# Self attention of a decoder layer: normalized tokens turned by way of memory and one VectorE turn

## The chip, the cores and the metric

The kernel runs on one core of a Trainium2 chip. The core has a matrix engine (TensorE, PE in the profile; its weight loads are listed as PEld), a vector engine (VectorE, DVE), an engine for activations and copies (ScalarE, ACT), a general engine (GpSimd, POOL) and an engine that issues transfers (SyncE, SP). Each works through its own instructions in order and waits on semaphores for the others. Tiles lie in on-chip memory of 128 partitions (SBUF); matrix products land in a second, small memory (PSUM), from which ACT or DVE must fetch them. Transfers between the chip's large memory and SBUF run on 16 DMA engines.

The metric is the device time of one execution in microseconds. Before the change it was 3776.5 us, the median of three runs (3776.08 to 3777.55).

## The reference

The program is one decoder layer in float32 over 32 batches of 128 tokens with 512 features: differential self attention, a cross attention, and a mixture of 32 experts with a shared expert. Only the first part is touched:

```python
x = x + attn(layernorm(x), Wq, Wk, Wv, Wo, lq1, lk1, lq2, lk2)
# attn: 16 heads, each with two halves of 16 features
q = (h @ Wq) * scaling; k = h @ Wk; v = h @ Wv      # h = layernorm(x)
aw = softmax(q k^T + causal)                        # 32 halves
aw = aw[first halves] - lam * aw[second halves]
out = rms_normalized(aw @ v) * (1 - LAMBDA_INIT) @ Wo
```

All three projections multiply the normalized tokens by weights, so they need the normalized tokens turned: features on the partitions, tokens along the free dimension (the tile `hT`).

## The kernel before

`self_attention` (L115) works in **steps**. A batch has two steps (`CP` = 2 of the four chunks of 128 features each); the loop at L478 runs step n over 64 (batch, half) pairs, with five more to drain. Every step holds pieces of several batches at once: for step n the maxima of the scores of step n (`maxima`), the exponentials of step n-1 (`turn_maxima`, `sums`, `exponentials`), the weighted values of step n-2 (`weigh`, `divide`), the projections of queries and keys for the next pair of batches (`queries_and_keys`, one of four chunks a step), and further pieces that alternate. In odd steps there are the projection to values for a later batch (`values`, L238 and the copy of v at L242) and, of batches two to three ahead, the shift by mean and deviation (`normalize`, L87 by way of `shifted`), the turn (`turn_in`, L199) and the next load of x (`load`, L151). In even steps there are the output projection (`leave`, L405, sum with x at L409, store at L410), the statistics of a later batch (`measure`: L56, L58, L60 on DVE, L62 and L66 on POOL), the mean squares of the heads (`norms`, L375 to L378) and the load of x for the residual (`load_again`, L398).

`turn_in` is done by TensorE: `turn4` takes a PSUM buffer, turns four 128 x 128 blocks against an identity (L95), and ACT copies the result to `hT` (L207). `hT` holds two batches and has two buffers. `queries_and_keys` (L220) and `values` (L238) read it.

All PSUM tiles come from one pool of four buffers (`banks`, L50), two banks each, handed out in the order of the claims: whoever claims a buffer waits until the last reader of the claim four earlier is done.

The order of the work: until `first.close()` (L476) every engine takes its instructions as written. Behind it a planner orders each engine's instructions: by their place in the program, among those that it takes to be ready by its own estimates of durations and transfers. The program can tie instructions with `tc.issue_after(ins)`: what is traced in that block on the engine of `ins` stays behind `ins` in that engine's order. `behind()` (L503) ties to the last reduction of the maxima (L264) of the step; `last_v` is the copy of v (L242). In the hardware each engine then keeps the planned order, whatever really comes late.

After self attention come the cross attention, its routing, the shared expert and the experts; their code stays as it is.

Of the kernel before, what the change touches and what calls it, by code (L numbers as in the profile page):

```python
# [10 lines left out]
F32 = mybir.dt.float32  # L11
# [7 lines left out]
P = 128  # L19
E = 512  # L20
EC = E // P
# [14 lines left out]
class Common:  # L36
# [49 lines left out]

        self.nc.scalar.activation(out, src, AF.Identity, bias=down, scale=rstd)  # L87

    def turn4(self, src, order=range(EC)):


        tr = self.banks()[:, 0, :].rearrange("p (c x) -> p c x", c=EC)
        cols = src.rearrange("p (c x) -> p c x", c=EC)
        for c, n in enumerate(order):
            self.nc.tensor.transpose(tr[:, c, :], cols[:, n, :], self.ident)  # L95
        return tr
# [15 lines left out]
            call(*args)  # L112


def self_attention(cm, x, x1_d, Wq, Wk, Wv, Wo, lq1, lk1, lq2, lk2, heads, heads_in, beside):  # L115

# [11 lines left out]
    nc, tc, bank = cm.nc, cm.tc, cm.banks  # L130
    B = x.shape[0]
    H, D, G = 16, 32, 2
    CP = 2
    ROW = (16, 0)
    with ExitStack() as ctx:
# [7 lines left out]
        pj2 = early.enter_context(tc.tile_pool(name="a_pj2", bufs=2))  # L143

        xin, xres = {}, {}

        def load(b, queue=nc.sync):

            if b < B:
                xin[b] = pj2.tile([P, E], F32, name="xin")  # L150
                queue.dma_start(out=xin[b], in_=x[b])  # L151
# [10 lines left out]
        for b in range(G):  # L162
            load(b, both[b % 2])
        w = {
            name: (wp if name == "wo" else pj).tile([P, EC, E], F32, name=name)
            for name in ("wk", "wq", "wv", "wo")
        }
        for oc in range(EC):
            for name, src, queue in (("wk", Wk, nc.sync), ("wq", Wq, both[oc < 2])):
                queue.dma_start(  # L170
                    out=w[name][:, :, ts(oc, P)],
                    in_=src[:, ts(oc, P)].rearrange("(c p) m -> p c m", p=P),
                )
            if oc == 0:
                nc.sync.dma_start(out=heads, in_=heads_in)
        vecs = wp.tile([P, 4, 16], F32, name="lam_vecs")
        for i, src in enumerate((lq1, lq2, lk1, lk2)):
            nc.sync.dma_start(out=vecs[:, i, :], in_=src.partition_broadcast(P))
        for name, src in (("wv", Wv), ("wo", Wo)):
            nc.sync.dma_start(out=w[name], in_=src.rearrange("(c p) m -> p c m", p=P))  # L180

        begun = wp.tile([P, 1], F32, name="a_begun")
        nc.scalar.activation(begun, cm.mhalf[:, 0:1], AF.Exp)
# [1 line left out]
        hT, qT, kz, k1, vs = {}, {}, {}, {}, {}  # L185
        last, last_v = {}, [None]
        h, sc_of, qm, expd, u, o, an = {}, {}, {}, {}, {}, {}, {}

        def measure(b):
            if b < B:  # L190
                h[b] = cm.moments(pj2, xin[b], "a_")

        def normalize(b):
            if b < B:
                rstd, down = h[b]
                h[b] = pj2.tile([P, E], F32, name="h")
                cm.shifted(h[b], xin.pop(b), rstd, down)

        def turn_in(b):  # L199

            if b >= B:
                return
            g, i = divmod(b, G)
            if i == 0:
                hT[g] = pj2.tile([P, EC, G * P], F32, name="hT")
            tr = cm.turn4(h.pop(b))
            nc.scalar.copy(hT[g][:, :, ts(i, P)], tr)  # L207

        def queries_and_keys(g, oc):

# [262 lines left out]
        for b in range(G):  # L473
            turn_in(G + b)
            load(2 * G + b)
        first.close()  # L476
        steps = [(b, cp) for b in range(B) for cp in range(EC // CP)]
        for n in range(len(steps) + 5):  # L478
            g, k = divmod(n, 2 * G)
            if n == len(steps) - 2 * G:  # L480
                early.close()
            at = {ago: steps[n - ago] for ago in range(6) if 0 <= n - ago < len(steps)}
            if 1 in at:
                turn_maxima(*at[1])
                sums(*at[1], 0)
            if 0 in at:
                maxima(*at[0])
            queries_and_keys(g + 1, k)
            if 1 in at:
                exponentials(*at[1])  # L490
                sums(*at[1], 1)
            if 2 in at:
                weigh(*at[2])
            if k % 2:
                values(g + 1, k // 2)
            elif 5 in at:
                leave(at[5][0])
            if 2 in at:
                divide(*at[2])
                if at[2][1]:  # L500
                    finish(at[2][0])

            def behind():  # L503

                return tc.issue_after(last[at[0]].ins) if 0 in at else nullcontext()

            b = (g + 2) * G + k // 2
            if k % 2 == 0:
                if 3 in at:
                    with behind():  # L510
                        norms(at[3][0])
                measure(b)
                if 4 in at:
                    load_again(at[4][0])
            else:
                normalize(b)
                turn_in(b)
                load(b + G)
                if 4 in at:
                    with behind():  # L520
                        scale_out(at[4][0])
                    turn_out(at[4][0])
            if n in beside:
                beside[n]()


class CrossAttention:
# [101 lines left out]
    def load(self, b):  # L629
        src = self.src  # L630
        src[b, "k"] = self.pi.tile([P, E], F32, name="cx")
        self.nc.sync.dma_start(out=src[b, "k"], in_=self.ctx_in[b])
        src[b, "q"] = self.pi.tile([P, E], F32, name="h2")
        self.nc.sync.dma_start(out=src[b, "q"], in_=self.x1_d[b])

    def measure(self, b):
        q = self.sided[b, "q", 0] = self.pi.tile([P, E], F32, name="xq0", bufs=2)
        self.scale[b] = self.cm.moments_by_sums(self.pi, self.src[b, "q"], q, "x_")
# [575 lines left out]
class Shared:  # L1214
# [4 lines left out]
    G = 4  # L1219
# [544 lines left out]
def decoder_kernel(  # L1764
# [5 lines left out]
    nc = tc.nc  # L1770
    B = x.shape[0]
# [14 lines left out]
    half_eid = const.tile([P, 2], I32, name="half_eid")  # L1786

    x1_d = dram.tile([B, P, E], F32, name="x1_d")
    h3_d = dram.tile([T, E], F32, name="h3_d")
    h3T_d = dram.tile([B, P, EC, P], F32, name="h3T_d")  # L1790
    table_ds = [dram.tile([(NX * B + 2) * P, 2], F32, name=f"table_d{i}") for i in range(2)]
# [6 lines left out]
    with tc.tile_pool(name="x_w", bufs=1, side="right") as x_w:  # L1798
        rest = x_w.tile([P, E], F32, name="rest")
        nc.gpsimd.memset(rest, 0.0)  # L1800
        routing = Routing(cm, x_w, table_ds, B)
        cross = CrossAttention(cm, x_w, x1_d, x2_d, h3_d, h3T_d, ctx_in, routing)
        cross.plan(lambda: s_w.load(), lambda: shared.load(0))
        x_ctx = ExitStack()

        def begin():
            cross.begin(
                x_ctx.enter_context(
                    tc.tile_pool(name="x_in", bufs=2, side="right", reuse_waits="tile")
                )  # L1810
            )
            cross.advance(7)

        n = 2 * B
        beside = {
            12: lambda: cross.load_weights(
                xWq, xbq, xWk, xbk, xWv, xbv, xWo, xbo, cos, sin, rotT, gate_w
            ),
            20: lambda: cross.prepare(heads),
            28: routing.prepare,  # L1820
            n - 4: begin,
        }

        for i, count in enumerate((4, 4, 5, 2, 2, 2, 2)):
            beside[n - 3 + i] = lambda count=count: cross.advance(count)
        self_attention(cm, x, x1_d, aWq, aWk, aWv, aWo, lq1, lk1, lq2, lk2, heads, heads_in, beside)
        s_w_pool = ctx.enter_context(tc.tile_pool(name="s_w", bufs=1, reuse_waits="tile"))
        s_w = SharedWeights(cm, s_w_pool, sw_gate, sw_up, sw_down)
        s_h_pool = ctx.enter_context(tc.tile_pool(name="s_h", bufs=2, reuse_waits="tile"))
        shared = Shared(cm, s_h_pool, h3T_d, sum_d, out)  # L1830
        x_out = ExitStack()
        p2 = x_out.enter_context(tc.tile_pool(name="x_p2", bufs=2, reuse_waits="tile"))
        cross.run(p2)
        x_ctx.close()
        s_pool = x_out.enter_context(tc.tile_pool(name="s_p", bufs=1, reuse_waits="tile"))
        shared.use(s_pool, s_w)
        en = mybir.EngineType
        in_order = {en.PE, en.DVE, en.Activation, en.Pool}
        todo = [lambda: cross.rest(2)] * 34 + [
            lambda: routing.tiles(eid, fresh, rows, used, usual, mixed),  # L1840
            lambda: routing.halves(half, half_eid),
            lambda: nc.sync.dma_start(out=sum_d[T : T + P, :], in_=rest),
        ]

        def between():
            if todo:
                todo.pop(0)()

        EARLY = 3
        with tc.manual_schedule(engines=in_order):
            for g in range(EARLY - 1):
                shared.group(g, False, between)
            while todo:
                between()
# [42 lines left out]
    for i in range(2):  # L1900
        b = done // 2
# [59 lines left out]
```

## Time and profile before

| what | us |
|---|---|
| median of 3 runs | 3776.5 |
| the profiled execution: time, span | 3776.16, 3774.4 |
| self attention, roughly | 0 to 750 |
| an odd and an even step (steps 7 to 56, but step 20) | 11.18 and 11.39 |
| steps 57, 58, 59 (no batch left to turn) | 10.75, 10.77, 10.75 |
| four turns on TensorE, start to the next work (L95) | 0.44 |
| copy of hT (L207), shift (L87) on ACT, each | 0.57, 0.81 |
| statistics of a batch on DVE (L56, L58, L60) | 0.69, 0.18, 0.15 |
| a turn of 32 x 32 blocks on DVE, 128 x 512 (L392) | 0.71 |

The length of a step is taken from the first L291 (the turn of the maxima, the first work of a step on TensorE) to the next step's. In the profile, busy time of an engine is the time that its instructions cover; the ends of matrix products are modelled, so a wait between two of them can hide in the busy time. Groups are named by line, engine, operation, and output and input tiles. "Idle before" is what the engine waited just before the instruction, and behind the arrow stands what ended the wait. The span is the time from the first to the last instruction of the program; the execution's own time is 1.8 us longer.

### The profile page before, as it was taken

To read this page: it belongs to the slowest core of one execution; us is meant where nothing else is said; L and a number is where in the kernel's file an instruction comes from. 1 tells how busy PE (TensorE), PEld (TensorE's weight loads), DVE (VectorE), ACT (ScalarE), POOL (GpSimd) and SP (SyncE) were. 2 spreads that over 40 slices of the span, in tenths; PEclk is the share of its full clock that TensorE was granted. 3 is DMA by queue.
4 is the path that set the end of the run, shared out by engine and by line. 5 is a ranking of instruction groups with operands and counts; after the bars stand their busy time and mean duration, and the time that the engine had idled before them with its cause. 6 is when DMAs were issued, how large, how long until landed. Compare 5 with 4: busy or idle time off the path is not lost. (4 is left out here: it accounts for less than half of the span.)

```text
span 3774.4 us, 62331 instructions
## 1 busy us (share of the span) xinstructions
PE 3693.1 (98%) x19828; PEld 1945.4 (52%) x19828; DVE 2600.8 (69%) x5594; ACT 2247.9 (60%) x6384; POOL 1921.4 (51%) x2154
## 2 busy tenths in 40 slices
PE   8999999889999999999999999999999999999999
PEld 5666666534444444444445555555555555555444
DVE  4888888877777878877425777777777777775111
ACT  6989999847667776766502555555555555554000
POOL 3555555545777777777423555555555555553000
PEclk9999999999999999999999999999999999999999
DMA  4111110121111111111125665656565665674210
GB/s 114 33 36 35 35 38 26 43 82 51 57 57 51 51 49 48 51 46 37 51 87 184 139 162 133 167 134 163 122 160 141 153 156 135 139 186 70 94 56 34
DMA packets 147715, 340.42 MB, mean 90 GB/s; under 512 B 28976, under 2 KB 33776, under 8 KB 147312
## 3 DMA queue, kind: packets, MB, share of 16 engines
q1 hardware_dynamic: 90560, 227.75, 18.6%
q0 software_dynamic: 55616, 107.79, 15.4%
q8 instruction: 160, 2.62, 0.3%
q14 instruction: 179, 1.47, 0.1%
q10 hardware_dynamic: 1200, 0.79, 0.1%
HBM read 574.59 MB, written 102.17 MB: 179 GB/s over the span
## 5 line engine op out<-in xcount | busy, mean ns | idle before, releaser
L694 DVE TENSOR_REDUCE nm<-ps 128x2 f32<-128x1024 f32 x512 | 611.0, 1215 | 113.1 <-PE ps L690 106.6
L717 ACT ACTIVATE xp<-ps 128x1024 f32<-128x1024 f32 x512 | 505.9, 1021 | 265.6 <-PE ps L690 203.0
L1688 POOL DMA_INDIRECT sum_d<-e_out,e_into x192 | 309.7, 1613 | 558.7 <-ACT e_out L1681 254.6
L713 PE MATMUL ps<-xqn,xk 32*128 32x512 f32 x2048 | 528.1, 621 | 20.6 <-ACT xp L717 19.2
L690 PE MATMUL ps<-xk,xq 32*128 32x512 f32 x2048 | 527.5, 631 | 0.8 <-DVE nm L694 0.7
L1593 DVE STREAM_TRANSPOSE e_xT<-e_xr 64x256 f32<-64x256 f32 x800 | 497.8, 622 | 17.4 <-issue 9.1
L1578 POOL DMA_INDIRECT e_xr<-h_d,e_run_of x400 | 415.2, 1038 | 161.1 <-issue 123.2
L1608 PE MATMUL ps<-wg,e_xT 128*128 128x352 f32 x1536 | 491.6, 463 | 0.0
L1608 PE MATMUL ps<-wu,e_xT 128*128 128x352 f32 x1536 | 485.7, 459 | 0.0
L1612 ACT ACTIVATE e_act<-ps 128x352 f32<-128x352 f32 x200 | 92.8, 464 | 575.2 <-PE ps L1608 553.8
L1608 PEld LDWEIGHTS ps<-wg,e_xT 128*128 128x128 f32 x1536 | 287.2, 190 | 229.3 <-issue 42.5
L278 ACT ACTIVATE s<-s,a_nm 128x128 f32<-128x128 f32 x1024 | 395.7, 395 | 5.1 <-DVE a_nm L264 5.1
L1649 ACT COPY e_mainT<-e_turned 32x64 f32<-32x64 f32 x1536 | 370.7, 241 | 20.2
L1643 DVE STREAM_TRANSPOSE e_mainT<-e_gu 32x64 f32<-32x64 f32 x1536 | 359.8, 234 | 24.6
L1608 PEld LDWEIGHTS ps<-wu,e_xT 128*128 128x128 f32 x1536 | 291.8, 190 | 162.6
L1660 PE MATMUL ps<-wd,e_mainT 128*128 128x512 f32 x768 | 361.9, 593 | 2.1 <-ACT e_mainT L1649 2.1
L1613 DVE TENSOR_TENSOR e_gu<-e_act,ps 128x352 f32<-128x352 f32 x200 | 104.2, 521 | 327.2 <-ACT e_act L1612 240.0
L713 PEld LDWEIGHTS ps<-xqn,xk 32*128 32x128 f32 x2048 | 169.1, 184 | 284.6 <-ACT xp L717 123.6
L728 PE MATMUL ps<-xp,v 128*32 128x512 f32 x2048 | 233.0, 595 | 7.9 <-ACT xp L717 7.4
L1031 POOL DMA_INDIRECT table_d<-entry,at x192 | 202.6, 1055 | 63.9 <-issue 53.1
L227 POOL TENSOR_SCALAR k<-kz,a_keep,a_extra 128x256 f32<-128x256 f32 x128 | 83.1, 659 | 286.8 <-ACT kz L226 286.8
L1272 ACT ACTIVATE s_act<-ps 128x512 f32<-128x512 f32 x40 | 23.9, 597 | 332.1 <-PE ps L1265 332.1
(315 smaller groups left out, 6189.9 us busy)
## 6 DMA issues: line engine op xcount, KB each, us to landing
wg<-in_L_ffn_w_gate_dram SPq DMA_DIRECT2D x192, 704.0 KB
wu<-in_L_ffn_w_up_dram SPq DMA_DIRECT2D x192, 704.0 KB
wd<-in_L_ffn_w_down_dram SPq DMA_DIRECT2D x192, 512.0 KB
wd_ends<-in_L_ffn_w_down_dram SPq DMA_DIRECT2D x192, 192.0 KB
xg<-in_L_ffn_w_gate_dram SPq DMA_DIRECT2D x16, 704.0 KB
xu<-in_L_ffn_w_up_dram SPq DMA_DIRECT2D x16, 704.0 KB
xd<-in_L_ffn_w_down_dram SPq DMA_DIRECT2D x16, 576.0 KB
xres<-in_x_dram SPq DMA_DIRECT2D x32, 256.0 KB
```

The source lines that it names most:

```text
L278: nc.scalar.activation(s[:, j, c, side, :], s[:, j, c, side, :], AF.Exp, bias=nm[n][:, side, at : at + 1], accum_out=sm[n][:, to : to + 1],)
L690: self.nc.tensor.matmul(sc[:, i, :], q[rows, ts(c, P)], k[rows, :], start=True, stop=True)
L694: self.nc.vector.tensor_reduce(at[:, self.ROW[side], 2 * pair : 2 * pair + 2], sc, AX.X, ALU.max, negate=True)
L713: self.nc.tensor.matmul(sc[:, i, :], k[rows, ts(c, P)], q[rows, :], start=True, stop=True)
L717: self.nc.scalar.activation(e, sc, AF.Exp)
L1578: self.cm.nc.gpsimd.indirect_dma_start(out=xr[:, t, :], out_offset=None, in_=self.h3_d.rearrange("t (h f) -> (t h) f", h=self.R), in_offse ...
L1593: self.cm.nc.vector.transpose(to[ts(w, half), :, v], xr[ts(v, half), w])
L1608: nc.tensor.matmul(pgu[lanes, half, 0:M], t[:, c, lanes], w[:, c, :], start=c == 0, stop=c == EC - 1,)
L1643: self.cm.nc.vector.transpose(t[ts(q, 32), 0:n, ts(s, 32)], cols[ts(s, 32)])
L1649: self.cm.nc.scalar.copy(t[ts(q, 32), 0:n, ts(s, 32)], z[ts(s, 32), k, 0:n])
L1660: mm(py, t[:, c, :], self.wd[i % SETS][:, c, :], start=c == 0, stop=False)
L1688: self.cm.nc.gpsimd.indirect_dma_start(out=self.sum_d[:, :], out_offset=bass.IndirectOffsetOnAxis(ap=into, axis=0), in_=y[:, :], in_offset ...
```

## The change

For batches 4 to 31 the turn no longer goes over TensorE. The shift (now in `send`) writes its result with two inner orders exchanged: of each 128 features, feature 4f + c goes to place 32c + f. The tile is stored to a new area `h_d` in memory and read back by four transfers, one for each 128 features and each into 32 partitions: partition 32q + i gets, for the four groups t of 32 tokens, the 128 features of quarter q of token 32t + i. One DVE instruction (`receive`) then turns each 32 x 32 block, and what comes out is `hT` with feature 4p + c on partition p in chunk c. So that this agrees with the weights, `wk`, `wq` and `wv` are now loaded with row 4p + c on partition p (`(p c) m` in place of `(c p) m`), and the first four batches, still turned on TensorE, are read with a step of four elements (`strided=True`).

The order changes too. `send(b + 1)` and its transfers stand in the odd step, tied on ACT behind the copy of v; `receive(b)` stands in the next even step, tied on DVE behind the maxima; the statistics `measure(b + 2)` move from the even to the odd step, tied on DVE behind the maxima; the load of x comes after the transfers of `send`. Before the loop, in the part that runs as written, the statistics of batches 4 and 5, the sending of batch 4 and a load are added.

```diff
-    def turn4(self, src, order=range(EC)):
+    def turn4(self, src, order=range(EC), strided=False):
...
-        cols = src.rearrange("p (c x) -> p c x", c=EC)
+        cols = src.rearrange("p (x c) -> p c x" if strided else "p (c x) -> p c x", c=EC)
...
-                    in_=src[:, ts(oc, P)].rearrange("(c p) m -> p c m", p=P),
+                    in_=src[:, ts(oc, P)].rearrange("(p c) m -> p c m", p=P),
...
-        for name, src in (("wv", Wv), ("wo", Wo)):
-            nc.sync.dma_start(out=w[name], in_=src.rearrange("(c p) m -> p c m", p=P))
+        nc.sync.dma_start(out=w["wv"], in_=Wv.rearrange("(p c) m -> p c m", p=P))
+        nc.sync.dma_start(out=w["wo"], in_=Wo.rearrange("(c p) m -> p c m", p=P))
...
-        def turn_in(b):
-
-            if b >= B:
-                return
+        def turned(b):
+
             g, i = divmod(b, G)
             if i == 0:
                 hT[g] = pj2.tile([P, EC, G * P], F32, name="hT")
-            tr = cm.turn4(h.pop(b))
-            nc.scalar.copy(hT[g][:, :, ts(i, P)], tr)
+            return hT[g][:, :, ts(i, P)]
+
+        def turn_in(b):
+            nc.scalar.copy(turned(b), cm.turn4(h.pop(b), strided=True))
+
+        def send(b):
+
+            if b >= B:
+                return
+            rstd, down = h[b]
+            t = pj2.tile([P, E], F32, name="h")
+            cm.shifted(
+                t.rearrange("p (q c f) -> p q f c", q=4, c=EC),
+                xin.pop(b).rearrange("p (q f c) -> p q f c", q=4, c=EC), rstd, down,
+            )
+            nc.sync.dma_start(out=h_d[b], in_=t)
+            h[b] = pj2.tile([P, 4, P], F32, name="h_runs")
+            for q in range(4):
+                nc.sync.dma_start(
+                    out=h[b][ts(q, 32)],
+                    in_=h_d[b][:, ts(q, P)].rearrange("(t i) r -> i t r", i=32),
+                )
+
+        def receive(b):
+
+            if b < B:
+                nc.vector.transpose(
+                    turned(b).rearrange("p c (t i) -> p c t i", i=32),
+                    h.pop(b).rearrange("p t (c f) -> p c t f", c=EC),
+                )
...
             turn_in(G + b)
             load(2 * G + b)
+        measure(2 * G)
+        send(2 * G)
+        load(3 * G)
+        measure(2 * G + 1)
         first.close()
...
-                measure(b)
+                with behind():
+                    receive(b)
                 if 4 in at:
                     load_again(at[4][0])
             else:
-                normalize(b)
-                turn_in(b)
-                load(b + G)
+                with tc.issue_after(last_v[0].ins):
+                    send(b + 1)
+                with behind():
+                    measure(b + 2)
+                load(b + 1 + G)
```

More of the change, by code (lines that the diff above doesn't have):

```diff
@@ L112, in run, with self_attention @@
             call(*args)
-def self_attention(cm, x, x1_d, Wq, Wk, Wv, Wo, lq1, lk1, lq2, lk2, heads, heads_in, beside):
+def self_attention(cm, x, x1_d, h_d, Wq, Wk, Wv, Wo, lq1, lk1, lq2, lk2, heads, heads_in, beside):
     nc, tc, bank = cm.nc, cm.tc, cm.banks
@@ L1788, in decoder_kernel @@
     x1_d = dram.tile([B, P, E], F32, name="x1_d")
+    h_d = dram.tile([B, P, E], F32, name="h_d")
     h3_d = dram.tile([T, E], F32, name="h3_d")
@@ L1825, in decoder_kernel @@
             beside[n - 3 + i] = lambda count=count: cross.advance(count)
-        self_attention(cm, x, x1_d, aWq, aWk, aWv, aWo, lq1, lk1, lq2, lk2, heads, heads_in, beside)
+        self_attention(cm, x, x1_d, h_d, aWq, aWk, aWv, aWo, lq1, lk1, lq2, lk2, heads, heads_in, beside)
         s_w_pool = ctx.enter_context(tc.tile_pool(name="s_w", bufs=1, reuse_waits="tile"))
```

## The prediction

> **What bounds the kernel now.** I read the page first, then stretches of self attention by engine, then its waits and its instructions in order of time. The page gives TensorE 98% of the span:
>
> ```profile
> PE 3693.1 (98%) x19828; PEld 1945.4 (52%) x19828; DVE 2600.8 (69%) x5594; ACT 2247.9 (60%) x6384; POOL 1921.4 (51%) x2154
> ```
>
> The chain that ended last covers only the last 290 us, so the stage has to be read by itself. Two steps of it (one batch), in the table by stretches; columns are length, then busy us of PE, PEld, DVE, ACT, POOL, then clock, DMA share, GB/s:
>
> ```profile
> 321.46:344.03 22.57, 22.57 (x187) 14.44 (x186) 18.88 (x28) 20.55 (x80) 11.60 (x13) 1.00 0.12 36
> ...
> 682.67:704.18 21.51, 21.51 (x183) 13.73 (x182) 18.14 (x25) 19.36 (x78) 10.94 (x11) 1.00 0.08 27
> ```
>
> PE has no gap in either. Each stretch runs from an odd step's first L291 to the next odd step's. In the first, which repeats with 22.57 us from step 7 to step 56 (step 20 apart, which holds other preparation), a batch is turned by PE; in the second no batch is left to turn, while projections, scores, values and output go on. So 21.51 us is what PE needs without the turn. The timeline of PE (start, length, line) shows where the 1.06 us lie:
>
> ```profile
> 306.19 3.60 PE L238 MATMUL ps<-wv,hT 128*128 128x512 f32 x8
> 309.63 0.60 PE L95 MATMUL ps<-ident,h 128*128 128x128 f32 x4
> 310.07 0.38 PE L291 MATMUL ps<-ident,a_nm 128*128 128x128 f32 x2
> 310.38 1.79 PE L251 MATMUL ps<-kz,qT 32*128 32x256 f32 x16
> 312.10 1.99 PE L220 MATMUL ps<-hT,wk 128*128 128x256 f32 x8
> ...
> 318.02 3.60 PE L405 MATMUL ps<-wo,anT 128*128 128x512 f32 x8
> 321.46 0.38 PE L291 MATMUL ps<-ident,a_nm 128*128 128x128 f32 x2
> 321.77 1.15 PE L251 MATMUL ps<-kz,qT 32*128 32x256 f32 x16
> ```
>
> The four turns take PE 0.44 us (309.63 to 310.07). Then the scores (L251) take 1.79 us instead of 1.15: the turn is a ninth claim on four PSUM buffers in a step that otherwise makes eight, so the scores wait for the copy of v and L220 for the copy of hT. Both copies, in ACT's timeline:
>
> ```profile
> 310.42 0.57 ACT L242 COPY v<-ps 128x512 f32<-128x512 f32 x1
> 310.88 0.64 ACT L368 ACTIVATE sq<-at 128x512 f32<-128x512 f32 x1
> 311.42 0.57 ACT L207 COPY hT<-ps 128x512 f32<-128x512 f32 x1
> ```
>
> hT ends at 311.99 and L220 starts at 312.10. "Busy" hides this wait, since a matmul's modelled end covers it.
>
> **The change part by part.** *Turns and hT copies leave.* 28 batches (4 to 31): 28 x 0.44 = 12.3 us of turns, 28 x 0.62 = 17.4 us of buffer waits; together 28 x 1.06 = 29.7 us. With eight claims a step, as in the second stretch, the scores wait for neither copy. ACT also loses 0.57 us a batch.
>
> *Moved on ACT: the shift.* It now follows the copy of v, hence (by program order) sq, at a step's border. It writes every 4 bytes to a new place 128 bytes on, which no ACT row shows. Low end 0.81 us (L87 as it is, and 0.80 in L87's other form, with two run orders exchanged); a gain below that I exclude, since the elements are as many. High end 1.44 us: L1593, a VectorE turn read 16 bytes apart, takes 630 ns for 256 elements, 2.46 ns each, against 711 ns for 512 at L392, 1.39 ns each: 0.81 x 1.77. I take 0.81, the same engine's row. The Trainium skill ("SBUF — State Buffer", section "Door 1: The DMA port swizzle") says that SBUF has 16-byte lines and that an access to a new line each time pays; it gives no price, so by it only the high end gains weight, and the L1593 row agrees in direction. Cover: ACT waits 2.02 us a batch for PE (before L226: 1.56 and 0.46), and in the second stretch's pattern 2.14 us; either end fits. Without that cover the shift costs PE its excess, up to 0.6 us a batch.
>
> *Moved on DVE: statistics.* L56, L58, L60 (0.69 + 0.18 + 0.15 = 1.03 us) go from the even step to the odd one, behind the maxima; behind them on DVE are an, anT, u and o, for which PE's buffers and POOL's L363 wait. In the second stretch DVE waits 0.94 us at the end of the odd step (L293 for L291), so it is 0.1 short; but the first o product takes 1.11 us there and 0.42 in the even step, and later it runs beside less of POOL's L318. I take 0; bounds 0 and 0.1 x 28 = 3 us. L56's wait for its load, 0.98 us here, goes, since that load now has two steps. POOL's two small operations (0.55 + 0.26) go along; POOL is idle half of the time.
>
> *Added on DVE: the turn.* L392 has its shape: 0.71 us; high end 2 x 0.63 = 1.26 if the exchanged order costs as at L1593; nothing below, it is the same work at least. I take 0.71, as both sides keep runs of 128 bytes. It comes in the even step, behind maxima and ms. DVE's busy time becomes 18.1 + 1.03 + 0.71 = 19.9 of 21.5 us.
>
> *Added on SP: one store and four reads, past x_d, xres and xin.* SP's waits show it idle most of the time, and what it issues has a step or more to spare (xres issued at 301.83 is used at 321.66). The chain counts: the store takes 2.03 us (L410 at 299.80; the load of xres that waits for it at 301.83), four issues 3 x 0.47 us (SP's issues at 8.91, 9.38, 9.86), the last read up to 2.46 us (L151 at 315.43, L56 starts 317.89): 5.9 us. Against an even step's L291 at 693.42: v ends +1.4, sq +1.9, shift +2.7, data +8.6 us. DVE reaches its turn at +6.9 (ms ends 700.31). If it waits there, the turn ends at +9.3 where u stood at +7.5: 1.8 us late. Behind u stand rs, o and L409, which waits 1.36 us for PE anyway:
>
> ```profile
> 700.95 0.85 DVE L339 STREAM_TRANSPOSE u<-ps 128x640 f32<-128x640 f32 x1 [0.43 <-PE ps L337]
> ...
> 702.54 0.48 DVE L352 SCALAR_TENSOR_TENSOR o<-u,nlam,rs 128x256 f32<-128x256 f32 x1
> 704.38 0.69 DVE L409 TENSOR_TENSOR xres<-xres,ps 128x512 f32<-128x512 f32 x1 [1.36 <-PE ps L405]
> ```
>
> So L409 is 0.4 us late, and PE needs its buffer only for L220 at 705.57, 0.5 us after it ends at 705.07: nothing is lost. If the planner puts the turn behind o, DVE does not wait. Bounds: 0, and with the shift at 1.44 us another 0.63, of which PE sees 0.55: 15 us. I take 1 us in all.
>
> *Start.* 16 turns now read 16 bytes apart, 3.3 us in all before: 0 more to 3.3 x 0.77 = 2.5; I take 1, between, as no PE row is near. Weights by "(p c)": wk and wq keep 512-byte runs; wv has landed when L238 starts right behind L220. Both 0. Shift and store of batch 4 come where ACT shifted it before (40.08). Steps 1 to 6 are irregular (70.8 us against 3 x 22.57): plus or minus 3 us, unpriced in the centre.
>
> The Trainium skill ("VectorE: DVE Perf Modes", section "Rules for kernel authors") speaks against the change: turn 128 x 128 on TensorE where PSUM may take the result. Taken as a time it would make the change cost 28 x (0.71 - 0.44) = 7.6 us. The row of PE without a gap decides otherwise: 0.71 us lie on an engine with waits.
>
> Sum: 29.7 - 1 - 1 = 27.7 us. The profiled execution took 3776.16 (span 3774.4 and 1.8 around it): 3748.5. It stands 0.3 under the median of 3776.5, so 3748.8.
>
> **Rivals.** (1) *The data come late and eat part of it.* As bounded above, 0.5 us a batch of PE wait behind L409: 14 us, 3763. For: L56 already waits 0.67 to 0.98 us for one load that the planner took to be there, and now there are two transfers in a row. Against: 1.36 + 0.5 us of slack. (2) *Slower: the shift falls behind the eight sums.* There it stood (L87 at 314.59, 4.5 us after L291) and data would be at 4.5 + 0.8 + 5.9 = 11.2. If the turn stays before u, it ends at +11.9, u is 4.4 late, L409 3.0, PE 2.5 us a batch: net 28 x (2.5 - 1.06) = 40 us, 3817. It decides once the data come after +9.7 (7.53 + 1.36 + 0.5 + 1.06 - 0.71), 1.1 us beyond my sum. Against: the statistics are now two steps old, so the shift is ready when v ends. (3) *Nothing is gained*, 3776: the steps without turn were short because statistics and shift were absent, too, and another engine takes PE's place. Against: ACT would have 20.0 and DVE 19.9 us in 21.5.
>
> **How the numbers follow.** Forecast 0.62 (3742 to 3753), rival 1 0.20 (3753 to 3769), rival 3 0.05, rival 2 0.13. A measurement tells about 0.2% (7.6 us) from no change, so faster is below 3769: 0.82; same 0.05; slower 0.13. For 8 in 10 the range goes from 3742, the early steps' 3 us and the start's costs on the good side, to 3770, through rival 1.
>
> **What would show it.** L291 to L291 of 10.75 in both steps; no L207 after the start; L251 at 1.15 in both; the shift right behind sq; the new turn at about 0.7 us and what DVE waits before it; L409's wait. Wrong if L220 of odd steps starts late behind L409 (rivals 1, 2), if ACT no longer waits before L226 (3), or if the shift is above 1.5 us.

## The result, and the profile after

The changed kernel takes 3815.85 us (median of 4 runs, 3814.38 to 3817.14), the kernel before 3776.73 beside it. The ratio is 1.0104, 95% interval 1.0091 to 1.0116: slower by 39 us. The forecast was 3748.8 us, the range 3742 to 3770. (Of all executions below, one of the kernel with the turn a step later took 6144.52 us at a granted clock of 0.556; the ratios leave it out.)

All of it lies in self attention: the first turn of the maxima (now L317) of step 57 starts at 723.82 us, before at 682.67, 41 us earlier. (Lines of the loop have moved by 26: L220 is L246, L251 L277, L318 L344, L352 L378, L405 L431, L409 L435. The new turn is L230, the store L219, the four reads L222.)

From the page, busy times of the engines; then one batch of the middle in the table by stretches (length, busy us of PE, PEld, DVE, ACT, POOL, clock, DMA share, GB/s):

```profile
PE 3677.3 (96%) x19716; PEld 1931.5 (51%) x19716; DVE 2659.2 (70%) x5622; ACT 2240.9 (59%) x6356; POOL 1916.7 (50%) x2154
```

```profile
507.00:531.31 24.31, 21.83 (x183) 13.80 (x182) 21.07 (x29) 20.29 (x79) 11.71 (x13) 1.00 0.18 56
```

TensorE works 21.83 us in the batch, less than the 22.57 of before, but the batch has become 24.31 us long: TensorE now has holes. The waits of the stretch from 120 to 640 us (total us, times, longest) name them:

```profile
DVE hT L230 <- DMA h_runs<-h_d: 54.0, 21, 3.6
...
POOL a_ln_rstd L62 <- DVE a_ln_ve L60: 33.5, 18, 2.0
...
PE ps L246 <- DVE xres L435: 30.0, 20, 1.6
ACT sq L394 <- POOL at L389: 26.6, 17, 1.6
...
PE ps L431 <- ACT qT L257: 14.5, 17, 0.9
```

VectorE waits for the turned-back data at L230 in front of the new turn, and TensorE then waits for L435, the sum with x. PE's timeline over the same batch shows where the two holes are, in the odd step (from 507.00) before L246 and in the even step (from 519.45) before L431:

```profile
507.31 1.15 PE L277 MATMUL ps<-kz,qT 32*128 32x256 f32 x16
510.09 1.99 PE L246 MATMUL ps<-hT,wk 128*128 128x256 f32 x8 [1.63 <-DVE xres L435]
...
519.45 0.38 PE L317 MATMUL ps<-ident,a_nm 128*128 128x128 f32 x2
519.76 1.15 PE L277 MATMUL ps<-kz,qT 32*128 32x256 f32 x16
...
527.79 3.70 PE L431 MATMUL ps<-wo,anT 128*128 128x512 f32 x8 [0.84 <-ACT qT L257]
```

What the change was to remove is gone: no turn on TensorE, and the scores (L277) take 1.15 us in both steps, in place of 1.79 in one. What came instead is read along the chain of the even step at 519.45, engine by engine. First POOL:

```profile
517.52 0.54 POOL L62 TENSOR_TENSOR a_ln_rstd<-a_ln_ve,mhalf 128x1 f32<-128x1 f32 x1 [1.75 <-DVE a_ln_ve L60]
518.17 0.26 POOL L66 TENSOR_SCALAR a_ln_down<-a_ln_mv,a_ln_rstd 128x1 f32<-128x1 f32 x1
518.38 2.33 POOL L344 TENSOR_SCALAR_AFFINE_SELECT e<-e 128x1024 f32<-128x1024 f32 x2
521.07 1.27 POOL L389 TENSOR_TENSOR at<-o 128x512 f32<-128x512 f32 x1 [0.36 <-DVE o L378]
```

The planner has put POOL's rstd (L62) ahead of the selects (L344; they set the masked exponentials to zero), and rstd waits 1.75 us for the variance that VectorE computes at 517.33. Before, rstd stood ahead of the selects too, but in the even step, with its input ready and no wait in front of it:

```profile
321.63 0.55 POOL L62 TENSOR_TENSOR a_ln_rstd<-a_ln_ve,mhalf 128x1 f32<-128x1 f32 x1
```

So in the changed kernel the two selects run at 518.38 to 520.71, beside VectorE's two products `o`:

```profile
517.33 0.11 DVE L60 TENSOR_SCALAR a_ln_ve<-a_ln_mv 128x1 f32<-128x1 f32 x1
...
518.52 1.24 DVE L378 SCALAR_TENSOR_TENSOR o<-u,rs 128x256 f32<-128x256 f32 x1
519.68 1.30 DVE L378 SCALAR_TENSOR_TENSOR o<-u,nlam,rs 128x256 f32<-128x256 f32 x1
...
527.04 0.17 DVE L402 TENSOR_SCALAR ms<-ms 128x16 f32<-128x16 f32 x1
530.17 0.71 DVE L230 STREAM_TRANSPOSE hT<-h_runs 128x512 f32<-128x512 f32 x1 [2.96 <-DMA h_runs<-h_d]
...
532.46 1.30 DVE L378 SCALAR_TENSOR_TENSOR o<-u,nlam,rs 128x256 f32<-128x256 f32 x1
533.68 0.68 DVE L435 TENSOR_TENSOR xres<-xres,ps 128x512 f32<-128x512 f32 x1
```

The products take 1.24 and 1.30 us; where no select runs they take 0.42 and 0.48. `at` on POOL follows at 521.07 to 522.34, and ScalarE's `sq`, which stands ahead of the shift in ScalarE's order, waits for it:

```profile
520.24 0.57 ACT L268 COPY v<-ps 128x512 f32<-128x512 f32 x1
...
522.37 0.63 ACT L394 ACTIVATE sq<-at 128x512 f32<-128x512 f32 x1 [1.56 <-POOL at L389]
522.90 1.28 ACT L87 ACTIVATE h<-xin,a_ln_down,a_ln_rstd 128x512 f32<-128x512 f32 x1
```

The shift itself takes 1.28 us and ends at 524.18, 4.7 us into the step. The store and the reads follow on SP's queue:

```profile
524.21 0.32 SPq L219 DMA_DIRECT2D h_d<-h  x1
...
526.22 2.23 SPq L222 DMA_DIRECT2D h_runs<-h_d  x4
```

The data are there at 530.17, 10.7 us into the step (10.2 to 11.4 in the batches whose shift is late like this one's). VectorE has had nothing to do since 527.21; the new turn, u and rs (the turned values and the reciprocals that the products take) and the products all come late, and L435 frees its PSUM buffer late, for which TensorE waits 1.6 us in the next odd step.

### The profile page after: what moved, and what is told of

Read it like the earlier page. It is cut to its first block, busy times and chain, and to the rows that moved or that the text cites. A ratio compares the mean times of both kernels' runs of the same rounds, so it can differ in the third digit from the quotient of the medians.

```text
span 3812.7 us, 62331 instructions
## 1 busy us (share of the span) xinstructions
PE 3677.3 (96%) x19716; PEld 1931.5 (51%) x19716; DVE 2659.2 (70%) x5622; ACT 2240.9 (59%) x6356; POOL 1916.7 (50%) x2154
## 5 line engine op out<-in xcount | busy, mean ns | idle before, releaser
L253 POOL TENSOR_SCALAR k<-kz,a_keep,a_extra 128x256 f32<-128x256 f32 x128 | 72.7, 578 | 328.5 <-ACT kz L252 328.5
```

## The experiments

Diffs are against the changed kernel unless said otherwise.

**The transfers taken away.**

```diff
-            nc.sync.dma_start(out=h_d[b], in_=t)
-            h[b] = pj2.tile([P, 4, P], F32, name="h_runs")
-            for q in range(4):
-                nc.sync.dma_start(
-                    out=h[b][ts(q, 32)],
-                    in_=h_d[b][:, ts(q, P)].rearrange("(t i) r -> i t r", i=32),
-                )
+            h[b] = t.rearrange("p (q x) -> p q x", q=4)
```

> Left out: the store to h_d and the four reads; the new VectorE turn reads the shifted tile directly, so tokens and features are mixed up in hT. All else is as in the changed kernel. Theory A (late data): VectorE's wait of 2.96 us a batch before its turn pushes u, the o products and the sum L435 late, and TensorE waits 1.63 us in the odd step for L435's buffer. Without transfers that wait goes: odd steps 12.45 to about 10.8, even steps stay near 11.9 or fall to 11.6, batch 24.33 to about 22.6, time 3764 to 3772. Theory B (statistics): the statistics in the odd step make POOL's rstd wait, push the select onto the o products and make sq and the shift late; the transfers matter little: time stays above 3800.

Measured: 3760.44 us, ratio to the kernel before 0.9958 (0.9944 to 0.9972). So 55 us of the changed kernel go with the transfers, whose data come late. The odd step is 10.74 to 10.78 us, but the even step still 11.5 instead of 10.77: a second cause stands in the even step that has nothing to do with the transfers.

**The turn one step later**, behind the maxima of the odd step, where the data have a whole step more.

```diff
-                with behind():
-                    receive(b)
                 if 4 in at:
...
                 with tc.issue_after(last_v[0].ins):
                     send(b + 1)
+                with behind():
+                    receive(b)
```

> The VectorE turn of a batch stands one step later, in the odd step behind the maxima and ahead of the statistics; transfers have some 11 us more. Theory A: VectorE's wait for the data goes, even steps end on time, TensorE no longer waits for L435; but the odd step now holds turn and statistics, 1.7 us more than before the change, against about 0.9 us of slack: batch about 22.6 to 23.2, time 3766 to 3785. Theory B: sq still waits 1.5 us for POOL, the shift stays late, and the time stays above 3800.

Measured: 3772.59 us, 0.9989 (0.9979 to 0.9999). No wait for the data is left, yet the even step takes 12.03 us: `sq` still waits 1.7 us for POOL's `at`, because rstd still waits ahead of the selects.

```profile
POOL a_ln_rstd L62 <- DVE a_ln_ve L60: 46.5, 23, 2.2
ACT sq L394 <- POOL at L389: 39.2, 23, 1.7
```

**The statistics back in the even step**, the turn left where the change put it.

```diff
-        measure(2 * G + 1)
...
+                with behind():
+                    measure(b + 1)
...
-                with behind():
-                    measure(b + 2)
```

> The statistics go back into the even step (those of the batch sent in the next odd step), tied behind the maxima; turn and transfers as changed. Theory B: POOL's select runs as before the change, the o products of the odd step fall from 1.24 and 1.30 to near 1.0 and 0.5 us, sq no longer waits for POOL, the shift ends 1.5 us sooner, data come 9.2 us after the even step's L317 instead of 10.7, VectorE arrives 1 us later and waits about 1.3 us instead of 2.96: batch about 22.2, time 3760 to 3772. Theory A alone, with the lateness not due to the statistics: data stay at 10.7 us, the wait falls only by the 1 us of statistics, batch above 23.5, time above 3795.

Measured: 3766.01 us, 0.997 (0.9959 to 0.9981). POOL's rstd and down again stand where they stood before, ahead of the selects but with their input ready, and `sq` waits no more. VectorE still waits 1.1 us a batch for the data (25.6 us in 23 batches), and single odd steps take 12.2 to 14.9 us; in the three of 14.9, TensorE's clock was also halved for 3.41 us (see the last section).

**Both: statistics in the even step, turn in the odd step.**

> Both: statistics in the even step, the VectorE turn a step later in the odd one. If A and B together are the whole loss, nothing is late: steps of 10.75 to 10.9, batch 21.5 to 21.8, time 3747 to 3756. If the shift's 1.28 us or the eight claims on PSUM cost TensorE on their own, the batch stays above 22.2 and the time above 3767.

Measured: 3742.03 us, 0.991 (0.9894 to 0.9927), with the whole computation. One batch in the table by stretches:

```profile
434.60:456.11 21.51, 21.51 (x184) 13.73 (x183) 18.81 (x29) 20.20 (x78) 11.43 (x13) 1.00 0.18 62
```

21.51 us, with no hole on TensorE: to the hundredth the stretch without a turn that the prediction took as the floor. So the expected gain was there to be had, and both moves in the order of the work kept the changed kernel from it. This kernel beats both.

**The shift in plain order**, first in the changed kernel, then in the kernel with both moves.

```diff
             cm.shifted(
-                t.rearrange("p (q c f) -> p q f c", q=4, c=EC),
-                xin.pop(b).rearrange("p (q f c) -> p q f c", q=4, c=EC), rstd, down,
+                t, xin.pop(b), rstd, down,
             )
```

> Left out: the exchange of the two inner orders in the shift's output, so hT's features do not agree with the weights. All else as in the changed kernel. Theory A with a share for the strided write: the shift falls from 1.28 to 0.81 us, data come 0.47 us sooner, and VectorE's wait, L435 and the copy of qT with them: batch 24.33 to between 23.4 and 23.9, time 3790 to 3803. If the strided write is hidden because something else sets the shift's end: time 3812 to 3818.

> As the run with statistics in the even step and the turn a step later, with the shift in plain order as in the last one (same part left out). There nothing waits for the shift, so ACT's 0.47 us a batch must cost nothing: 3740 to 3744. If TensorE still waits for ACT somewhere, up to 13 us less.

Measured: 3806.45 us, 1.0079 (1.0062 to 1.0096), and 3741.93 us, 0.9909 (0.9893 to 0.9926). The shift falls from 1.28 to 0.80 us. In the changed kernel this gives 9.4 us, and of the 0.48 the even step shows 0.36 (11.89 to 11.53); with both moves it gives nothing, since ScalarE has the time.

**The order of GpSimd alone.** rstd and down are issued only behind `at`; within self attention the orders of the other four engines are the same, instruction for instruction, as in the changed kernel (this one), and likewise those of VectorE and ScalarE as with the turn one step later (the other one, which has both edits).

```diff
-    def moments(self, pool, src, tag=""):
+    def moments(self, pool, src, tag="", half=False):
...
+        if half:
+            return mv, ve
+        return self.scales(pool, mv, ve, tag)
...
-            nc.gpsimd.tensor_tensor(
+            last_at[0] = nc.gpsimd.tensor_tensor(
...
+                if n:
+                    with tc.issue_after(last_at[0].ins) if last_at[0] else nullcontext():
+                        scale(b + 1)
...
-                    measure(b + 2)
+                    measure(b + 2, True)
```

> The changed kernel with only this change of POOL's order; the turn stays in the even step. Theory B: sq and shift come 1.5 us sooner, data 9.2 us after L317, VectorE still waits about 2 us, L435 is about 1 us late, batch about 22.2 to 22.6: time 3760 to 3775. Rival C: sq stays late, time above 3800.

> The kernel with the turn a step later (statistics in the odd step on VectorE) with one thing more: POOL's two operations of the statistics, rstd and down, stand behind its sum of the heads (at) instead of ahead of the selects. VectorE's and ACT's orders are the same as there. Theory B, POOL's order: the selects no longer wait for the statistics, the o products do not run beside them, at and sq are on time, TensorE no longer waits for the copy of qT: even steps 12.03 to 10.8, time 3742 to 3750. Rival C, VectorE's own time: the odd step holds 1.0 us of statistics more on VectorE whatever POOL does, o is late anyway, and the time stays at 3765 to 3773.

Measured: 3780.87 us, 1.0016 (1.0006 to 1.0025), for the order alone, and 3753.17 us, 0.9938 (0.9921 to 0.9954), with the turn a step later. Two small operations behind instead of ahead of the selects are worth 35.0 and 19.4 us. In the first of the two kernels, VectorE (whose lines have moved by 11):

```profile
496.21 0.42 DVE L389 SCALAR_TENSOR_TENSOR o<-u,rs 128x256 f32<-128x256 f32 x1
496.55 0.48 DVE L389 SCALAR_TENSOR_TENSOR o<-u,nlam,rs 128x256 f32<-128x256 f32 x1
...
506.54 0.71 DVE L241 STREAM_TRANSPOSE hT<-h_runs 128x512 f32<-128x512 f32 x1 [2.16 <-DMA h_runs<-h_d]
...
508.73 1.31 DVE L389 SCALAR_TENSOR_TENSOR o<-u,nlam,rs 128x256 f32<-128x256 f32 x1
```

The products of the odd step fall back to 0.42 and 0.48, since the select is over; VectorE's order has not changed, so it is the select that made them slow. In this batch the data now come 9.4 us into the even step (which starts at 497.14), and TensorE still waits 1.33 us (1.24 in most batches):

```profile
510.69 1.99 PE L257 MATMUL ps<-hT,wk 128*128 128x256 f32 x8 [1.33 <-DVE xres L446]
```

In the kernel with the turn a step later, 11 us are left against both moves. There the even step is 11.27, and VectorE's `an` takes 1.54 us beside a select, instead of 0.68. It starts 0.09 us behind the select (493.26), right after the turn and L56, which stand ahead of it in VectorE's order, so the statistics that VectorE now carries in the odd step push it there. That is the part that rival C of that expectation has:

```profile
493.35 1.54 DVE L421 SCALAR_TENSOR_TENSOR an<-at,rr 128x512 f32<-128x512 f32 x1
```

**GpSimd's order and the plain shift together**, to see what the remaining 1.33 us are made of. The diff is the two above.

> This is the changed kernel with the two edits together that were tried apart: the order of GpSimd in which rstd and down stand behind at, and the shift written in plain order (features in their own places, so that hT holds other features than the weights expect: the output is not the reference's, and nothing else is left out). It tests how the 1.33 us are made up that TensorE still waits in each even step with GpSimd's order alone (3780.9 us). Theory A: the wait is the sum of two things that the prediction did not have, the shift's excess of 0.48 us (1.30 in place of 0.81) and the second o product beside GpSimd's select, 0.83 us (1.31 in place of 0.48), both behind the prediction's slack of 1.36 + 0.5 us, which is used up. Then this kernel still waits 1.33 - 0.48 = 0.85 us a batch, and the time is 3780.9 - 28 x 0.48 = 3767 us (3764 to 3771), with o nlam still near 1.3 us in even steps. Theory B: the late data alone make the wait, and the collision is a by-product, gone as soon as u comes a little earlier; then the wait falls by more than the shift's excess, o nlam is near 0.5 us, and the time comes to 3743 to 3756 us. Theory C: the shift is not on the path here: 3777 to 3783.

Measured: 3760.03 us, 0.9962 (0.9949 to 0.9974), between what A and B expected; 20.8 us less than with the odd writes. The reason for the miss is in the lengths: the odd steps are no longer alike. Of the 24 from step 9 to 55, eleven take 11.90 to 11.98 us and thirteen 10.78 to 10.96, and nothing lies between. VectorE's data, products and L445 in three batches, whose even steps start at 457.05, 479.73 and 502.42:

```profile
465.34 0.71 DVE L240 STREAM_TRANSPOSE hT<-h_runs 128x512 f32<-128x512 f32 x1 [1.19 <-DMA h_runs<-h_d]
...
467.18 1.31 DVE L388 SCALAR_TENSOR_TENSOR o<-u,rs 128x256 f32<-128x256 f32 x1
468.42 1.30 DVE L388 SCALAR_TENSOR_TENSOR o<-u,nlam,rs 128x256 f32<-128x256 f32 x1
...
488.79 0.71 DVE L240 STREAM_TRANSPOSE hT<-h_runs 128x512 f32<-128x512 f32 x1 [1.96 <-DMA h_runs<-h_d]
...
490.64 0.54 DVE L388 SCALAR_TENSOR_TENSOR o<-u,rs 128x256 f32<-128x256 f32 x1
491.10 1.30 DVE L388 SCALAR_TENSOR_TENSOR o<-u,nlam,rs 128x256 f32<-128x256 f32 x1
...
510.51 0.71 DVE L240 STREAM_TRANSPOSE hT<-h_runs 128x512 f32<-128x512 f32 x1 [0.99 <-DMA h_runs<-h_d]
...
512.35 0.42 DVE L388 SCALAR_TENSOR_TENSOR o<-u,rs 128x256 f32<-128x256 f32 x1
512.70 1.31 DVE L388 SCALAR_TENSOR_TENSOR o<-u,nlam,rs 128x256 f32<-128x256 f32 x1
```

And POOL's selects of the same batches:

```profile
467.12 2.32 POOL L354 TENSOR_SCALAR_AFFINE_SELECT e<-e 128x1024 f32<-128x1024 f32 x2
...
489.81 2.32 POOL L354 TENSOR_SCALAR_AFFINE_SELECT e<-e 128x1024 f32<-128x1024 f32 x2
...
512.49 2.47 POOL L354 TENSOR_SCALAR_AFFINE_SELECT e<-e 128x1024 f32<-128x1024 f32 x2
```

In the first batch the data come 8.29 us into the step, the first product starts 0.06 us after the first of the two selects and takes 1.31; in the second they come at 9.06, and the product, started 0.83 us after the select, takes 0.54. They end 11.44 and 11.45 us into the step. The first of the two selects ends at 11.17, so a product that starts while it runs ends 0.27 us after it, whenever it started: it is held until the select is over. (One batch's product, started at 11.09 with the select almost done, took its usual 0.43.) In the third batch the data come at 8.09, the first product starts 0.14 us ahead of the select and takes 0.42; only the second waits. So what a late turn costs TensorE has a step in it: little (10.84) where the first product is ahead of the select, 1.08 us more (11.92) where it is behind, and much the same for data at 8.29 (11.92) as at 9.25 (11.98).

The edge lies between data at 8.21 and at 8.29. Eleven of the 24 batches missed it, because their reads were issued later than at 4.66 (in four, at 4.85 to 5.66), or because the reads took longer with the issue at the usual 4.6 to 4.7 (six, all with a fetch of instructions among the transfers just then), or for both (one). In the six the fetch began 4.7 to 6.6 us into the step; four batches in time had one too, but theirs began at 7.4 to 7.7. In the four whose reads were issued late a fetch began at 2.5 to 3.2, about when the store began. So a fetch goes with the delay in all eleven, but two batches in time had one near the store as well (2.6 to 2.8), and no run tried the fetches apart: the cause stays open.

## Why the prediction was wrong

**Right.** The turn and the copies of hT cost 1.06 us a batch and no more is lost to them: 21.51 us with both moves. The new turn takes 0.71. Store and reads take 5.99 us from the shift's end in the batch shown, 5.4 to 6.8 over the batches from step 6 on; predicted 5.9. v's copy ends 1.36 us into the step, predicted 1.4. L56 waits for no load. The start costs nothing (L317 begins at 44.80, the kernel before 45.44; predicted 1 us), and with both moves the six steps from 1 on (70.80 before, 64.54) give 3 us more than the 3.2 priced, within the 3 that were left open. So that kernel ends 6.8 us below the forecast.

**The step that failed first: "Moved on DVE: statistics ... I take 0".** The three instructions cost VectorE little by themselves. But the text disposed of their followers with "POOL's two small operations ... go along; POOL is idle half of the time". A half idle engine still has an order: rstd stands ahead of the selects, waits 1.75 us for VectorE, and the selects wait with it. No sentence named POOL's queue behind that wait. The price was 35.0 us with POOL's order alone put right (the transfers taken away gave 55, some of it from the other terms). The same paragraph carried the row that should have warned: "the first o product takes 1.11 us there and 0.42 in the even step". It was read as time that the change would give back ("beside less of POOL's L318"), and not as a rule that a select holds the product up wherever they meet; the change made them meet more. The mean of the second product in self attention shows it, in the kernel before, then after (lines by form, 120 to 640 us and 120 to 690 us; total us and mean ns):

```profile
L352 DVE SCALAR_TENSOR_TENSOR o<-u,nlam,rs 128x256 f32<-128x256 f32 x46 | 21.8, 475 | 0.0
```

```profile
L378 DVE SCALAR_TENSOR_TENSOR o<-u,nlam,rs 128x256 f32<-128x256 f32 x47 | 55.5, 1180 | 0.0
```

The Trainium skill ("SBUF — State Buffer", section "Who interferes with whom") states what these rows are: a VectorE instruction with two inputs in SBUF and a GpSimd instruction that reads SBUF use one port between them, and the one that starts first keeps the other out until it ends. The products and `an` have two such inputs, and the runs agree: 0.42 us alone, up to 1.31 behind a select, with the end 0.27 us after the select's.

**The second term: "sq +1.9, shift +2.7, data +8.6".** Measured +3.5, +4.7 and +10.7 in the batch shown. Of the 2.1 us, 1.56 are `sq`'s wait for the late `at`, and 0.47 the shift, taken at 0.81 and measured at 1.28 (within its bounds, near the upper). The row it was taken from writes in order; the one that was far away, a strided turn on another engine, was the better guide. With POOL's order right this excess was worth 20.8 us, in the changed kernel as it is 9.4, with both moves nothing: its price is set by what is late behind it.

**The third: "L409 is 0.4 us late ... nothing is lost".** The slack was computed as if everything behind u kept its duration, 1.36 us in front of L409 and 0.5 behind it. But in the same step of the kernel before the products end at 703.02 and POOL's selects start at 703.48:

```profile
702.20 0.42 DVE L352 SCALAR_TENSOR_TENSOR o<-u,rs 128x256 f32<-128x256 f32 x1
```

```profile
703.48 2.14 POOL L318 TENSOR_SCALAR_AFFINE_SELECT e<-e 128x1024 f32<-128x1024 f32 x2
```

The first product, at 702.20, may be 1.28 us late, the second, at 702.54, 0.94, before they fall behind a select. The forecast's own u was 1.8 us late. So with everything as forecast, data at +8.6, both products would have waited for the selects, and TensorE 1.08 us a batch (11.92 against 10.84): 28 x 1.08 = 30 us, all of the gain. For 28 batches this is worked out, not measured; the edge that it rests on, 8.21 to 8.29, is, and two batches of the kernel with POOL's order and the plain shift had data at +8.5: their odd steps took 11.91 us.

**The rivals.** Rival 2 gave 3817 us for data that come late while the turn stands before u, and 3815.85 was measured, but its cause did not happen: the shift did not fall behind the eight sums, it stood behind `sq`, as forecast. The agreement of the numbers is in part chance: the lateness was 10.7, not the 11.2 us of that text, and the break-even was 8.2 to 8.3, not 9.7. Rival 1 had the place, but its price for late data (0.5 us a batch) left out the selects. The kernel that comes closest to what the prediction assumed, with POOL's order and the plain shift, takes 3760.03 us, within rival 1's 3753 to 3769; there 11 of 24 batches pay 1.1 us and the others little. Rival 3 is refuted by the 21.51 us. With 0.13 for the slower side, the two ways of being late, on a chain of five transfers and three engines with a slack of one microsecond, were priced far too low.

**The account.** From the changed kernel, in this order: POOL's order 3815.85 to 3780.87, 35.0 us; the shift's excess, to 3760.03, 20.8; the turn moved behind the data and the statistics back in their step, to 3741.93 (both moves and plain shift), 18.1. In another order the parts have other sizes. The kernel before, measured beside each of these kernels, took 3775.5 to 3776.7 us, so a part is known to about 1 us at best.

## What to carry to other kernels

When an instruction moves, write down for each engine that it feeds what stands behind it in that engine's queue: an engine that is half idle still makes everything behind a waiting instruction wait. Before a slack is counted as free, look at which work on the other engines the late instructions slide into; here a product that started 0.2 us later, behind a GpSimd select in place of ahead of it, took 0.9 us longer. A turn that goes by way of memory belongs in a place a whole step behind its transfers; with that and the statistics left where they were, the change is worth 0.9% (0.991, 0.9894 to 0.9927).

## What was not expected of the hardware

- The price of lateness has a step: in the kernel with POOL's order and the plain shift, data 8.21 us into the step or earlier cost TensorE at most 0.22 us in the next odd step (against 10.74 with both moves), data at 8.29 to 9.25 all cost 1.16 to 1.24.
- ScalarE's shift of 128 x 512 takes 0.80 us with its results side by side, and 1.28 to 1.32 where each 4 bytes go to a place 128 bytes on.
- The way of 256 KB to memory and back in another shape, a store and four reads, took 5.4 to 6.8 us from the end of the producer to the start of the consumer in the changed kernel. In the kernel with POOL's order and the plain shift the data came 8.06 to 9.25 us into the step.
- TensorE's clock fell to half at some of the holes. With the statistics in the even step, L246 took 3.67 us instead of 1.99 after a wait of 2.40; the table by stretches shows a granted clock of 0.50 for 3.41 us there. The length of the wait alone does not decide it: in the changed kernel the same followed waits of 1.38, 1.52 and 1.64 us, and did not follow 21 others of 1.18 to 1.64. There it made an odd step 1.7 us longer (14.35 against 12.66), but the next even step then took 10.77 instead of 11.89 and the next odd step 12.1 instead of 12.45, so most of it came back.

```profile
204.36 3.67 PE L246 MATMUL ps<-hT,wk 128*128 128x256 f32 x8 [2.40 <-DVE xres L435]
```

```profile
204.38:207.79 3.41, 3.41 (x8) 2.78 (x9) 3.38 (x5) 0.00 (x0) 0.00 (x0) 0.50 0.25 90
```
